# VectorE and ScalarE in program order through the MLP of a transformer block, with the next tokens' normalisation split in three

## The chip, the core and the metric

The kernel runs on one core of a Trainium2 chip. The core has a matmul engine (TensorE, "PE" in the profile; its weight loads stand apart as "PEld"), three engines for elementwise work (VectorE "DVE", ScalarE "ACT", GpSimd "POOL") and SyncE ("SP"), which here only issues transfers. The engines run side by side, each through its own list of instructions in order, and wait for each other on semaphores. The metric is the device time of one execution in microseconds (us), the median of several runs; lower is better. Before the change it is 2831.77 us (three runs, 2831.14 to 2831.92).

## The reference

Two layers on an image of 48 x 48 positions with 768 channels, in float32. The first is a transformer block with 12 heads of attention (with relative positions by row and column) and an MLP with 3072 inner channels; the second goes to frequencies, applies two small complex layers in blocks of 96 channels, and comes back.

```python
xn = layernorm(x); q, k, v = split(xn @ qkv_w + qkv_b)
attn = softmax(q * scale @ k.T + rel_h + rel_w)
x = x + (attn @ v) @ proj_w + proj_b
xn2 = layernorm(x, ln2_g, ln2_b)                 # over the 768 channels
h = gelu(xn2 @ mlp_w1 + mlp_b1)                  # 768 -> 3072
x = x + (h @ mlp_w2 + mlp_b2)                    # 3072 -> 768
xf = rfft2(x); ...; y = irfft2(z) + x            # second layer
```

The change touches the MLP (from `xn2` to the end of the first layer) alone.

## The kernel before

**Tokens and steps.** The 2304 tokens lie in SBUF as 18 tiles of 128 tokens (`x1`, called `main` in the profile). The MLP goes over them in three parts `p` of 768 tokens (`TB`), and in each part over 12 steps `n` of 256 inner channels (`FCH`). Every product of 2 x 2 blocks is computed with seven block products in place of eight (a Winograd form of Strassen's scheme), which needs sums of blocks: of tokens (`sums_of_tokens`, line 179, written to `shared`), of weights (`left` and `right` on GpSimd, lines 161 to 170, `w1s` and `w2s`) and of inner channels (`left` on VectorE, lines 161 to 164, `hs` and a rewritten quarter of `hT`).

**One step on TensorE.** `hidden(p, n)` makes the inner channels of step n: seven products (line 1291) of three matmuls each, into four PSUM banks `h0` to `h3`, cut by `yield` in three pieces of 2, 2 and 3 products. `added(p, n-1, i)` adds the step before to the result for token tiles i = 0, 1, 2: seven products (lines 1355 and 1351) into banks `o0` to `o3`. The two are interleaved: a piece of `hidden(p, n)`, then `added(p, n-1, i)`, three times. Each float32 matmul of this kernel runs as two passes, so the profile has two rows where the code has one call.

**What follows each product.** In `hidden`: a copy `m1` on ScalarE (L1310), the sums `u`, `u7` and `c` on VectorE (L1303, named `u` and `c`), four Gelus on ScalarE (L1297), and then `left` on VectorE (L161 to L164). In `added`, VectorE adds each bank to an accumulator `acc` or to `x1` (L1357, L1359, L1353). Inside one `added`, three banks are used a second time: the fifth product waits until VectorE has read `o0` (the first add), the sixth until it has read `o2` (the third add), the seventh until it has read `o3` (the fourth). The second product needs line 162's result, the third needs line 164's.

**Next tokens.** `normalised(p + 1, i)`, i = 0 to 5, prepares the tokens of the next part: two `bn_stats` (L123) and `bn_aggr` (L125) on VectorE, a square root on ScalarE (L127), a reciprocal (L128) and the scaled copy `hat` (L131) on VectorE, and on GpSimd the second layer's bias is added to `x1` (L1407). In program order the six stand at steps 4 to 9. After step 11, `turned(piece)` transposes a third of the hats on TensorE (L1415) and evacuates them on ScalarE (L1416) ahead of each `added(p, 11, i)`; then come `sums_of_tokens`, the next weights, and `rows_forward(p)` (L1383, `zp`), which starts the second layer's transform.

**Who sets the order.** Through the MLP the order of TensorE, GpSimd and SyncE is that of the program text (`manual_schedule`). VectorE and ScalarE are left to a list scheduler, which places each instruction by priority and by its own costs, and may put it earlier or later than the text has it, across steps and parts. In the built program it does: the six normalisations of part 1 stand at the very start of the MLP, in steps 0 to 2 of part 0, those of part 2 around the end of part 0 (the first statistics of them at the start too), and the pieces of `sums_of_tokens` between the adds of `added(p, 11, 2)`.

```python
work = hidden(p, n)
for i in range(3):
    next(work)
    if n:
        added(p, n - 1, i)
if n < n_f - 1 and (p == 0 or n):
    weights(p, n + 1)
if p < 2 and 4 <= n < 10:
    normalised(p + 1, n - 4)
```

Of the kernel before, what the change touches and what calls it, by code (L numbers as in the profile page):

```python
# [10 lines left out]
F32 = mybir.dt.float32  # L11
F32R = mybir.dt.float32r
I32 = mybir.dt.int32
AF = mybir.ActivationFunctionType
ALU = mybir.AluOpType
# [4 lines left out]
P = 128  # L20
# [3 lines left out]
C = 768  # L24
# [22 lines left out]
def block_then_afno(  # L47
# [27 lines left out]
    nc = tc.nc  # L75
# [10 lines left out]
    eps = const.tile([P, 1], F32, name="eps")  # L86
# [32 lines left out]
    def normalise(pool, src, hat=None, made=None):  # L119

        stats = pool.tile([P, 2, 6], F32, name="stats")
        for i in range(2):
            nc.vector.bn_stats(stats[:, i, :], src[:, ts(i, C // 2)])  # L123
        mv = pool.tile([P, 2], F32, name="mv")
        nc.vector.bn_aggr(mv, stats.rearrange("p a b -> p (a b)"))  # L125
        rstd = pool.tile([P, 1], F32, name="rstd")
        nc.scalar.activation(rstd, mv[:, 1:2], AF.Sqrt, bias=eps)  # L127
        nc.vector.reciprocal(rstd, rstd)  # L128
        if hat is None:
            hat = pool.tile([P, C], F32, name="hat", bufs=4)  # L130
        last = nc.vector.tensor_scalar(hat, src, mv[:, 0:1], rstd, ALU.subtract, ALU.mult)  # L131
        if made is not None:
            made.append(last)
        return hat
# [25 lines left out]
    def left(eng, a11, a12, a21, a22, s):  # L160
        eng.tensor_tensor(s[0], a21, a22, ALU.add)  # L161
        eng.tensor_tensor(s[1], s[0], a11, ALU.subtract)  # L162
        eng.tensor_tensor(s[2], a12, s[1], ALU.subtract)
        eng.tensor_tensor(a21, a11, a21, ALU.subtract)  # L164
# [30 lines left out]
    with ExitStack() as flag_scope:  # L195
# [810 lines left out]
        with tc.If(safe < 1):  # L1006
            with ExitStack() as att:
                xnT = main.rearrange("p (c t) -> p c t", c=NC)
                with tc.tile_pool(name="g_ln1", bufs=3) as ln1, tc.tile_pool(
                    name="g_ps_ln1", bufs=2, space=PSUM  # L1010
                ) as psum:
                    for g in range(T // G):
                        hats = []
# [230 lines left out]
    with ExitStack() as mlp:  # L1244
# [15 lines left out]
        def weights(p, n):  # L1260

            w = wpool.tile([P, NC, FCH], F32, name="w1")
            nc.sync.dma_start(
                out=w, in_=mlp_w1[:, ts(n, FCH)].rearrange("(c p) f -> p c f", p=P)
            )
            ws = wpool.tile([P, 3, 3, P], F32, name="w1s")
            a11, a12, a21, a22 = (w[:, ds(3 * j, 3), ts(i, P)] for i in range(2) for j in range(2))
            left(nc.gpsimd, a11, a12, a21, a22, [ws[:, i] for i in range(3)])
            v = wpool.tile([P, 2, C], F32, name="w2")
            nc.sync.dma_start(  # L1270
                out=v, in_=mlp_w2[ts(n, FCH), :].rearrange("(j p) c -> p j c", p=P)
            )
            vs = wpool.tile([P, 3, CH], F32, name="w2s")
            right(
                nc.gpsimd, v[:, 0, :CH], v[:, 0, CH:], v[:, 1, :CH], v[:, 1, CH:],
                [vs[:, i] for i in range(3)],
            )
            ready_w[p, n] = a11, a12, a21, a22, ws, v, vs

        def hidden(p, n):  # L1280

            a11, a12, a21, a22, ws, v, vs = ready_w.pop((p, n))
            h = hpool.tile([P, 2, TB], F32, name="hT")
            hs = hpool.tile([P, 3, G], F32, name="hs", bufs=1)
            kept[p, n] = h, hs, v, vs

            bank = [psum.tile([P, G], F32, name=f"h{i}") for i in range(4)]

            def product(i, a, b, start):
                for c in range(3):  # L1290
                    nc.tensor.matmul(  # L1291
                        bank[i], a[:, c, :], b[:, c, :],
                        start=(start and c == 0), stop=(c == 2), skip_group_check=not start,
                    )

            def gelu(i, k, src):
                nc.scalar.activation(  # L1297
                    h[:, i, ts(k, G)], src, AF.Gelu, bias=col(V_B1 + 2 * n + i)
                )

            def summed(src, other, name, bufs=2):
                t = upool.tile([P, G], F32, name=name, bufs=bufs)
                nc.vector.tensor_tensor(t, src, other, ALU.add)  # L1303
                return t

            b11, b21, t3, b22, t1, t2, t4 = parts_of_tokens(xt, xs)
            s1, s2, s4 = (ws[:, i] for i in range(3))
            product(0, a11, b11, True)
            m1 = upool.tile([P, G], F32, name="m1")
            nc.scalar.copy(m1, bank[0])  # L1310
            product(1, s2, t2, True)
            u = summed(bank[1], m1, "u")
            yield
            product(2, a21, t3, True)
            u7 = summed(bank[2], u, "u7")
            product(3, s1, t1, True)
            gelu(1, 1, summed(bank[3], u7, "c", 3))
            yield
            product(0, a12, b21, False)
            gelu(0, 0, bank[0])  # L1320
            product(2, a22, t4, False)
            gelu(1, 0, summed(bank[2], u, "c", 3))
            product(3, s4, b22, False)
            gelu(0, 1, summed(bank[3], u, "c", 3))
            left(
                nc.vector, h[:, 0, :G], h[:, 1, :G], h[:, 0, G:], h[:, 1, G:],
                [hs[:, i] for i in range(3)],
            )
            yield
# [3 lines left out]
        def added(p, n, i):  # L1333

            h, hs, v, vs = kept[p, n]
            bank = [psum.tile([P, CH], F32, name=f"o{k}") for k in range(4)]
            if n == 0:
                acc[i] = upool.tile([P, CH], F32, name=f"acc{i}", bufs=1)
            a11, a12, s3, a22 = (
                h[:, f, ds(k * G + i * P, P)] for f, k in ((0, 0), (1, 0), (0, 1), (1, 1))  # L1340
            )
            s1, s2, s4 = (hs[:, k, ts(i, P)] for k in range(3))
            b11, t3, b21, b22 = (v[:, f, ts(k, CH)] for f in range(2) for k in range(2))
            t1, t2, t4 = (vs[:, k] for k in range(3))
            t = 2 * (p * 3) + i
            x11, x12, x21, x22 = (
                x1[:, t + 3 * j, ts(k, CH)] for j in range(2) for k in range(2)
            )

            def product(k, a, b, start, *into):  # L1350
                nc.tensor.matmul(bank[k], a, b, start=start, stop=True, skip_group_check=not start)  # L1351
                for dst in into:
                    nc.vector.tensor_tensor(dst, bank[k], dst, ALU.add)  # L1353

            nc.tensor.matmul(bank[0], a11, b11, start=True, stop=True)  # L1355
            if n == 0:
                nc.vector.tensor_copy(acc[i], bank[0])  # L1357
            else:
                nc.vector.tensor_tensor(acc[i], bank[0], acc[i], ALU.add)  # L1359
            product(1, s2, t2, True, acc[i])  # L1360
            product(2, s3, t3, True, x22)
            product(3, s1, t1, True, x22)
            product(0, a12, b21, False, x11)
            product(2, a22, t4, False, x21)
            product(3, s4, b22, False, x12)
            if n == n_f - 1:
                nc.vector.tensor_tensor(x21, x21, acc[i], ALU.add)
                nc.gpsimd.tensor_tensor(x12, x12, acc[i], ALU.add)
                nc.gpsimd.tensor_tensor(x22, x22, acc[i], ALU.add)
# [29 lines left out]

        hats = {}  # L1400

        def normalised(p, i):

            t = 6 * p + i
            hats[i] = turn.tile([P, C], F32, name="hat2", tag="turn")
            normalise(upool, x1[:, t, :], hats[i])
            nc.gpsimd.tensor_tensor(x1[:, t, :], x1[:, t, :], b2, ALU.add)  # L1407

        def turned(piece):
# [8 lines left out]
                )  # L1418

        weights(0, 0)  # L1420
        for p in range(T // TB):
            for n in range(n_f):
                if (p, n) == (0, 2):
                    nc.sync.dma_start(out=b2, in_=mlp_b2[0, :].partition_broadcast(P))
                    nc.sync.dma_start(out=rows_dft, in_=c_rows)
                work = hidden(p, n)
                for i in range(3):
                    next(work)
                    if n:
                        added(p, n - 1, i)  # L1430
                if n < n_f - 1 and (p == 0 or n):
                    weights(p, n + 1)
                if p < 2 and 4 <= n < 10:
                    normalised(p + 1, n - 4)
            for i in range(3):
                if p < 2:
                    turned(i)
                added(p, n_f - 1, i)
            if p < 2:
                sums_of_tokens(xt, xs)  # L1440
                for n in range(2):
                    weights(p + 1, n)
            rows_forward(p)
        in_order.close()

    with ExitStack() as sp:
# [382 lines left out]
```

## Time and profile before

| what | value |
|---|---|
| median of three runs | 2831.77 us (2831.14 to 2831.92) |
| the profiled execution | 2834.65 us |
| its span, first to last instruction | 2832.9 us |
| TensorE busy in the span | 2788.5 us (98%) |
| VectorE, ScalarE, GpSimd busy | 1700.6, 920.6, 668.7 us |
| mean granted TensorE clock | 0.996 |
| the MLP, first matmul of L1291 to last of L1383 | 1554.4 to 2590.0 us |
| one step of the MLP in the middle of a part | 27.1 us |
| L161 to L164 on VectorE, 144 instructions | 83.3 us busy |
| L1353, adds to `x1` and second adds to `acc` | 358.9 us busy, 556 ns each |

The profile's times are from one execution under the profiler. A row of a timeline gives the start in us from the start of the span, the time from the first start to the last end of the rows merged in it, engine, line, operation, what is written and read, and how many (x). In square brackets stands how long the engine was idle before it and what ended that. The busy end of a matmul is modelled and lies some 0.16 us behind the start of the next one when they follow each other without a gap, so a stall of TensorE is read best from starts: in free running the two passes of a 384 column product take 0.645 us from one product's start to the next.

### The profile page before, as it was taken

To read this page: it belongs to the slowest core of one execution; us is meant where nothing else is said; L and a number is where in the kernel's file an instruction comes from. 1 tells how busy PE (TensorE), PEld (TensorE's weight loads), DVE (VectorE), ACT (ScalarE), POOL (GpSimd) and SP (SyncE) were. 2 spreads that over 40 slices of the span, in tenths; PEclk is the share of its full clock that TensorE was granted. 3 is DMA by queue.
4 is the path that set the end of the run, shared out by engine and by line. 5 is a ranking of instruction groups with operands and counts; after the bars stand their busy time and mean duration, and the time that the engine had idled before them with its cause. 6 is when DMAs were issued, how large, how long until landed. Compare 5 with 4: busy or idle time off the path is not lost. (4 is left out here: it accounts for less than half of the span.)

```text
span 2832.9 us, 41042 instructions
## 1 busy us (share of the span) xinstructions
PE 2788.5 (98%) x15759; PEld 1716.2 (61%) x15759; DVE 1700.6 (60%) x2520; ACT 920.6 (32%) x1466; POOL 668.7 (24%) x662
## 2 busy tenths in 40 slices
PE   8999999999999999999999999999999999999998
PEld 4555655656656565665555555555555555556887
DVE  5434236767676767676756756565565566566665
ACT  1101135656566565665401201131101201102332
POOL 2505010000000000000164233342242422222432
PEclk9999999999999999999999999999999999999999
DMA  4535375273664737455332112131121212123254
GB/s 149 182 103 162 106 158 111 58 133 69 105 126 65 132 64 133 85 82 99 110 132 79 53 65 67 45 101 56 45 67 62 95 45 67 45 70 108 62 162 142
DMA packets 218430, 269.09 MB, mean 95 GB/s; under 512 B 24645, under 2 KB 197053, under 8 KB 216689
## 3 DMA queue, kind: packets, MB, share of 16 engines
q1 hardware_dynamic: 215720, 264.33, 37.5%
q8 instruction: 127, 2.08, 0.3%
q10 hardware_dynamic: 2440, 1.84, 0.2%
q14 instruction: 79, 0.64, 0.1%
q0 software_dynamic: 64, 0.20, 0.0%
HBM read 150.25 MB, written 52.32 MB: 72 GB/s over the span
## 5 line engine op out<-in xcount | busy, mean ns | idle before, releaser
L689 ACT ACTIVATE main<-sp 128x768 f32<-128x768 f32 x648 | 516.3, 812 | 34.5 <-PE sp L679 19.6
L833 DVE TENSOR_TENSOR pairs<-pairs,main 128x1536 f32<-128x1536 f32 x252 | 443.0, 1758 | 27.1 <-DVE pairs L833 0.9
L679 PE MATMUL sp<-terms,select 64*128 64x384 f32 x1296 | 412.0, 629 | 0.0
L1353 DVE TENSOR_TENSOR main<-o,main 128x384 f32<-128x384 f32 x540 | 298.7, 556 | 39.3 <-PE o L1351 1.2
L1291 PE MATMUL h<-shared,w 128*128 128x384 f32 x864 | 296.6, 486 | 0.7 <-POOL w2s L167 0.7
L670 PE MATMUL sp<-shared 64*128 64x384 f32 x1296 | 265.2, 485 | 1.6 <-ACT row_hi L241 1.0
L670 PE MATMUL sp<-qT,kT 64*128 64x384 f32 x1296 | 264.1, 484 | 0.0
L1291 PEld LDWEIGHTS h<-shared,w 128*128 128x128 f32 x864 | 163.9, 190 | 116.1 <-POOL w2s L167 1.3
L735 POOL TENSOR_TENSOR inverse<-inverse,rden 24x32 f32<-24x32 f32 x36 | 15.1, 421 | 926.5 <-DVE sums L734 887.5
L1291 PE MATMUL h<-shared,w1s 128*128 128x384 f32 x648 | 226.6, 486 | 0.0
L1297 ACT ACTIVATE hT<-c,vec 128x384 f32<-128x384 f32 x108 | 66.5, 615 | 465.1 <-DVE c L1303 465.0
L702 PE MATMUL op<-main,shared 128*64 128x384 f32 x1296 | 217.4, 488 | 0.0
L702 PE MATMUL op<-main,v 128*64 128x384 f32 x1296 | 216.4, 488 | 0.0
L833 DVE TENSOR_TENSOR pairs<-main 128x1536 f32<-128x1536 f32 x36 | 63.3, 1758 | 248.1 <-ACT main L689 248.1
L1303 DVE TENSOR_TENSOR c<-h,u 128x384 f32<-128x384 f32 x108 | 60.1, 557 | 212.4 <-PE h L1291 212.4
L1351 PE MATMUL o<-w,hT 128*128 128x384 f32 x432 | 174.8, 487 | 2.4 <-DVE mv L125 2.0
L1351 PE MATMUL o<-w2s,hs 128*128 128x384 f32 x432 | 174.9, 487 | 1.6 <-DVE hs L162 1.6
L679 PEld LDWEIGHTS sp<-terms,select 64*128 64x128 f32 x1296 | 125.3, 186 | 83.7
L1291 PEld LDWEIGHTS h<-shared,w1s 128*128 128x128 f32 x648 | 123.1, 190 | 85.8
L167 POOL TENSOR_TENSOR w2s<-w 128x384 f32<-128x384 f32 x36 | 35.9, 998 | 566.0 <-DMA w<-in_mlp_w_dram 424.0
L529 PE MATMUL m<-main 128*128 128x384 f32 x504 | 164.6, 488 | 2.4 <-DVE main L179 1.8
L702 PEld LDWEIGHTS op<-main,v 128*64 128x64 f32 x1296 | 96.9, 137 | 92.7 <-issue 67.7
(209 smaller groups left out, 4136.6 us busy)
## 6 DMA issues: line engine op xcount, KB each, us to landing
w<-in_mlp_w_dram SPq DMA_DIRECT2D x72, 768.0 KB
terms<-col_parts SPq DMA_DIRECT2D x432, 72.0 KB
terms<-row_hi SPq DMA_DIRECT2D x216, 72.0 KB
terms<-row_lo SPq DMA_DIRECT2D x216, 72.0 KB
main<-in_qkv_w_dram SPq DMA_DIRECT2D x36, 384.0 KB
z<-zt SPq DMA_DIRECT2D x48, 192.0 KB
x<-in_x_blocks_dram SPq DMA_DIRECT2D x18, 384.0 KB
k_d<-o SPq DMA_DIRECT2D x36, 192.0 KB
```

The costliest lines, as they stand in the source:

```text
L167: eng.tensor_tensor(t[0], b12, b11, ALU.subtract)
L529: nc.tensor.matmul(bank, a[:, c, :], b[:, c, :], start=(first and c == 0), stop=(c == 2), skip_group_check=not first,)
L670: nc.tensor.matmul(sp[:, j, :G], kT[at, ts(kt, P)], qT[at, ts(c, G)], start=first, stop=not first,)
L679: nc.tensor.matmul(sp[:, j, :G], select[at, a % 2], ready[pr, c][at, a // 2, b], start=first, stop=not first,)
L689: nc.scalar.activation(p, sp[:, :, :G], AF.Exp, scale=HD**-0.5)
L702: nc.tensor.matmul(op[ts(j, 64)], v[:, kt, ts(j, 64)], exps[:, kt, j, :], start=(kt == 0), stop=(kt == NT - 1),)
L833: nc.vector.tensor_tensor(pairs, so_far, exps[:, ds(kt - 1, 2)], ALU.add)
L1291: nc.tensor.matmul(bank[i], a[:, c, :], b[:, c, :], start=(start and c == 0), stop=(c == 2), skip_group_check=not start,)
L1297: nc.scalar.activation(h[:, i, ts(k, G)], src, AF.Gelu, bias=col(V_B1 + 2 * n + i))
L1303: nc.vector.tensor_tensor(t, src, other, ALU.add)
L1351: nc.tensor.matmul(bank[k], a, b, start=start, stop=True, skip_group_check=not start)
L1353: nc.vector.tensor_tensor(dst, bank[k], dst, ALU.add)
```

## The change

Three edits in the MLP, all of them in the order of work. First, the loop over the parts now stands in `manual_schedule` for VectorE and ScalarE too, so that they run in the order of the text. Second, `hidden` has a fourth piece: `left` on VectorE, which stood ahead of the third `yield`, stands behind it, and `next(work)` is called a fourth time after `added(p, n-1, 2)`; in the text the sums of the inner channels so come behind the adds of the last token tile. Third, `normalised` is cut up: `measured` (statistics, at steps 3 to 8, one tile a step, into one tile `mv6` for all six), one square root for the six at the end of step 8, and from step 9 to 11 two `hat`s a step, the first of them behind one reciprocal for the six. The bias adds on GpSimd go with the hats, two each at steps 9, 10 and 11.

In the built program, TensorE and SyncE have the same instructions in the same order as before. GpSimd has the same instructions, with the twelve bias adds at their new places. VectorE and ScalarE have the order of the text, except that three VectorE instructions of the second layer's setup (L1489 to L1491) still stand among the adds of part 2, where they stood before.

```diff
--- before.py
+++ after.py
@@ -1322,6 +1322,7 @@
             gelu(1, 0, summed(bank[2], u, "c", 3))
             product(3, s4, b22, False)
             gelu(0, 1, summed(bank[3], u, "c", 3))
+            yield
             left(
                 nc.vector, h[:, 0, :G], h[:, 1, :G], h[:, 0, G:], h[:, 1, G:],
                 [hs[:, i] for i in range(3)],
@@ -1399,11 +1400,33 @@
 
         hats = {}
 
+        measures = {}
+
+        def measured(p, i):
+
+            if i == 0:
+                measures[p] = [
+                    upool.tile([P, 6, 2], F32, name="mv6", bufs=1),
+                    upool.tile([P, 6], F32, name="rstd6", bufs=1),
+                ]
+            stats = upool.tile([P, 2, 6], F32, name="stats")
+            for k in range(2):
+                nc.vector.bn_stats(stats[:, k, :], x1[:, 6 * p + i, ts(k, C // 2)])
+            nc.vector.bn_aggr(measures[p][0][:, i], stats.rearrange("p a b -> p (a b)"))
+            if i == 5:
+                mv, rstd = measures[p]
+                nc.scalar.activation(rstd, mv[:, :, 1], AF.Sqrt, bias=eps)
+
         def normalised(p, i):
 
             t = 6 * p + i
+            mv, rstd = measures[p]
+            if i == 0:
+                nc.vector.reciprocal(rstd, rstd)
             hats[i] = turn.tile([P, C], F32, name="hat2", tag="turn")
-            normalise(upool, x1[:, t, :], hats[i])
+            nc.vector.tensor_scalar(
+                hats[i], x1[:, t, :], mv[:, i, 0:1], rstd[:, i : i + 1], ALU.subtract, ALU.mult
+            )
             nc.gpsimd.tensor_tensor(x1[:, t, :], x1[:, t, :], b2, ALU.add)
 
         def turned(piece):
@@ -1418,6 +1441,10 @@
                 )
 
         weights(0, 0)
+        part_by_part = ExitStack()
+        part_by_part.enter_context(
+            tc.manual_schedule(engines={mybir.EngineType.DVE, mybir.EngineType.Activation})
+        )
         for p in range(T // TB):
             for n in range(n_f):
                 if (p, n) == (0, 2):
@@ -1428,10 +1455,14 @@
                     next(work)
                     if n:
                         added(p, n - 1, i)
+                next(work)
                 if n < n_f - 1 and (p == 0 or n):
                     weights(p, n + 1)
-                if p < 2 and 4 <= n < 10:
-                    normalised(p + 1, n - 4)
+                if p < 2 and 3 <= n < 9:
+                    measured(p + 1, n - 3)
+                if p < 2 and n > 8:
+                    for i in range(2 * (n - 9), 2 * (n - 8)):
+                        normalised(p + 1, i)
             for i in range(3):
                 if p < 2:
                     turned(i)
@@ -1441,6 +1472,7 @@
                 for n in range(2):
                     weights(p + 1, n)
             rows_forward(p)
+        part_by_part.close()
         in_order.close()
 
     with ExitStack() as sp:
```

## The prediction

> **What bounds the kernel now.** I read the page first: TensorE is busy 98% of the span, so the change can only win what TensorE loses by waiting, and the question is how much of that lies in the MLP.
>
> ```profile
> PE 2788.5 (98%) x15759; PEld 1716.2 (61%) x15759; DVE 1700.6 (60%) x2520; ACT 920.6 (32%) x1466; POOL 668.7 (24%) x662
> ```
>
> Second, the waits of TensorE between 1554 and 2592 us, the MLP (who waits, for whom, total us, times, longest): little, and nearly all of it for VectorE.
>
> ```profile
> PE o L1351 <- DVE main L1353: 3.5, 5, 1.6
> PE o L1351 <- DVE mv L125: 2.0, 1, 2.0
> PE o L1351 <- DVE hs L162: 1.6, 2, 1.1
> PE h L1291 <- POOL w2s L167: 0.7, 1, 0.7
> PE o L1351 <- DVE hT L164: 0.4, 1, 0.4
> ```
>
> Third, windows from the start of one `added` to the start of what follows it (edges, length, busy us by engine, clock, DMA). An `added` is seven products at 0.645 us, 4.52 us; what a window has over that is lost.
>
> ```profile
> 1571.85:1580.74 8.89, 5.83 (x16) 2.25 (x15) 8.89 (x16) 2.72 (x6) 4.47 (x4) 1.00 0.01 2
> 1877.51:1883.01 5.50, 5.05 (x17) 2.44 (x16) 5.50 (x12) 3.34 (x6) 2.57 (x2) 1.00 0.01 1
> 1884.32:1891.20 6.88, 5.24 (x17) 2.23 (x15) 6.80 (x9) 1.58 (x3) 2.84 (x2) 0.99 0.00 0
> 1891.20:1905.82 14.62, 14.62 (x81) 6.00 (x80) 9.09 (x16) 7.68 (x17) 12.83 (x11) 0.89 0.67 230
> 2230.45:2236.57 6.12, 5.15 (x17) 2.32 (x15) 6.04 (x9) 1.58 (x3) 4.21 (x2) 1.00 0.00 0
> 2236.57:2249.62 13.05, 13.05 (x82) 5.63 (x81) 4.01 (x4) 7.19 (x15) 11.19 (x11) 1.00 0.73 258
> 2546.42:2551.58 5.16, 4.78 (x15) 2.54 (x14) 4.76 (x9) 0.61 (x1) 0.00 (x0) 1.00 0.32 92
> 2561.90:2567.76 5.86, 4.76 (x16) 2.57 (x15) 5.39 (x12) 0.00 (x0) 0.00 (x0) 1.00 0.02 4
> ```
>
> VectorE fills the bad windows: it is late there, not slow on average. Lost, with 0.09 us off where `zp` follows (that step from 0.645 us also costs it with no wait): start 8.89 − 4.52 = 4.4; end of part 0: 1.0 + 2.3; the `zp` run behind it 14.62 − 13.05 = 1.6, at clock 0.89 against 1.00 in part 1; end of part 1: 1.5; part 2: 0.6 + 1.3. Together 12.7 us, the ceiling. Between these, steps follow at 27.1 us without a gap.
>
> **What makes VectorE late.** At the start, hoisted normalisations and `left`, both stretched beside GpSimd's weight sums:
>
> ```profile
> 1571.85 1.23 DVE L162 TENSOR_TENSOR hs<-hs,hT 128x384 f32<-128x384 f32 x1
> 1573.01 1.35 DVE L164 TENSOR_TENSOR hT<-hT 128x384 f32<-128x384 f32 x1
> 1574.28 1.34 DVE L163 TENSOR_TENSOR hs<-hT,hs 128x384 f32<-128x384 f32 x1
> ```
>
> Around the end of part 0, free-running `left` (0.47 us from start to start), hats, and token sums placed in front of adds:
>
> ```profile
> 1870.61 0.56 DVE L161 TENSOR_TENSOR hs<-hT 128x384 f32<-128x384 f32 x1 [0.16 <-PE o L1351]
> 1871.09 0.55 DVE L1353 TENSOR_TENSOR main<-o,main 128x384 f32<-128x384 f32 x1
> 1871.56 0.55 DVE L162 TENSOR_TENSOR hs<-hs,hT 128x384 f32<-128x384 f32 x1
> 1872.02 0.55 DVE L164 TENSOR_TENSOR hT<-hT 128x384 f32<-128x384 f32 x1
> 1872.49 0.55 DVE L163 TENSOR_TENSOR hs<-hT,hs 128x384 f32<-128x384 f32 x1
> ...
> 1877.29 1.94 DVE L131 TENSOR_SCALAR hat<-main,mv,rstd 128x768 f32<-128x768 f32 x2
> 1879.15 0.55 DVE L1359 TENSOR_TENSOR acc<-o,acc 128x384 f32<-128x384 f32 x1
> ...
> 1886.69 1.68 DVE L179 TENSOR_TENSOR shared<-shared 128x1152 f32<-128x1152 f32 x1
> ```
>
> **The change, part by part.** Let T be the end of `added(p, n-1, 2)` on TensorE (1870.34 above).
>
> *Start.* No normalisation is left in steps 0 to 2. Step 0 ends at 1554.36 + 21 x 0.645 = 1567.9; its `c` (0.55), Gelu (0.61) and four `left` (0.47 apart) end near 1571.4, as GpSimd's next weights land (1571.36), and `added(0, 0, 0)`, 6 x 0.645 us behind, needs line 162 at 1572.4. Saves 4.4.
>
> *`left` behind the adds.* In every step the last add (L1353) and L161 change places, as do L163 and L164, so L162 stays at T+1.22 and L164 ends at T+2.70, 0.47 later. TensorE first runs 3.87 us of `hidden` and needs L164 at T+5.16: hidden, with 2.4 us to spare. Without that cover, at the end of part 2, 2561.90 + 2.70 + 0.05 for the semaphore is 0.12 behind the third product's 2564.53; with 0.1, which the trace adds after each stall, +0.2.
>
> *Statistics, steps 3 to 8.* Two L123 and one L125 take 1.1 us (1566.07 to 1567.14), from T+2.6 to T+3.7. Next on VectorE is `u`, due at T+3.98 (1946.72 to 1950.70): nothing. The cover is 0.3 us; a late `u` would push the adds, which have 0.5 to 0.8 us before a bank's second use stalls TensorE.
>
> *One square root, end of step 8.* On ScalarE it waits for the statistics (T+3.7) ahead of `m1`, so `m1` moves from T+2.03 to about T+4.1 and `u` from T+3.98 to T+4.65. The adds start 0.55 late; the first ends at T+5.67 and is needed at T+6.45, the third at T+6.6 and T+7.1. Nothing. Its table load (1.28 us, as in L127's) and Gelu's stand on a ScalarE that has no Gelu before T+12. The ten square roots saved are on an engine 10 to 20% busy: nothing beyond the start.
>
> *Hats, steps 9 and 10.* Reciprocal 0.15 and two hats, 0.67 each when alone, T+2.6 to T+4.0; GpSimd's weight sums come at T+4.8 (1951.55). Nothing. The bias adds (1.80 us each) go on GpSimd behind `w2s`, T+8.8 to T+12.4, ahead of the next `w1s`, then done by T+16.5 and due at T+27.1: nothing.
>
> *Hats, step 11 of parts 0 and 1.* Here TensorE has only 1.31 us of transposes before `added(p, 11, 0)`. Products start at T+1.31, 1.96, then the third waits for L164 (2.75 for 2.63), the fourth at 3.5. Hats run at T+2.62 and T+3.20; the adds follow. What the second hat costs, no row shows exactly: 0.67 alone, 1.36 when GpSimd was already waiting. GpSimd's bias add is released by the first hat's end (T+3.29), when the second has started, which is nearest to the first of two hats at 1895.65, 0.77, which was running when GpSimd's L161 began (1895.96). I take 0.67. The first add ends at T+4.34, so the fifth product starts at 4.39 in place of 4.14; the third add ends at T+5.28, so the sixth at 5.33 in place of 5.13. Sum 0.12 + 0.25 + 0.2 and three times 0.1: 0.9 us an end. With 1.36 it is 1.6. GpSimd's two bias adds then end by T+7.6; the accumulator adds behind them are not needed before `zp`.
>
> By the Trainium skill ("SBUF — State Buffer", section "Who interferes with whom") VectorE and GpSimd hold a shared port pair for a whole instruction, first come first served. By that rule the second hat keeps the pair, 0.67, and the sum is as taken; the stretched rows 1.23 to 1.36 agree with it.
>
> *Token sums.* They now stand behind all adds of `added(p, 11, 2)`: 4 x 1.35 us behind T', its end, due when `hidden(p+1, 0)` needs them, T' + 13.05 + 1.9. Cover 8 us. This frees the adds: the 1.0 + 2.3 and the 1.5 go, for 0.9 each.
>
> *Clock behind the stall.* Between 1891.0 and 1894.4 the granted clock was 0.5, after 1.62 us of idle TensorE; 0.95 us at the end of part 1 and 2.00 at the start brought none. With stalls below 0.4 us I expect none: 1.6 saved. By the skill ("TensorE: Matmul & The Clock Gate", "What's actually happening") the clock falls after an idle window of about 3.4 us; here 1.62 sufficed, so the trace differs, and by the rule alone this saving would not follow and the sum would be 7.0.
>
> *Sum.* 12.7 lost before; after 0 + 0.9 + 0.9 + 2.1 (1.9 and 0.2) is 3.9, so 8.8 saved; I take 8.6 for small change at the seams. The profiled execution had 2834.65, giving 2826.05; it stood 2.88 above the median, which gives 2831.77 − 8.6 = 2823.2. Bounds: no stall at the part ends, −1.8, 2821.4; both second hats at 1.36, +1.4, 2824.6; and if the runs without profiler had no slow clock to lose, +1.6, 2826.2.
>
> **Rivals.**
> (1) *Given back at the part ends* (0.18). Hats at 1.36 and a granted clock of 0.5 behind both: 2 x (0.7 + 1.6) = 4.6, so 2827.8. For: all VectorE work of the end is in one queue. Against: 1.6 us in pieces, in a trace where 0.95 brought no drop.
> (2) *Swallowed* (0.08). Behind the MLP TensorE waits for ScalarE, GpSimd and DMA (chain from 2590 on); if one of these has its own date, the end stays: 2831.8. Against: all of them follow from `zp`, and their order is unchanged.
> (3) *Slower: `left` meets GpSimd* (0.07). Behind the adds, `left` might run beside the weight sums, at 1.25 us: from T+0.75 to T+5.75, 0.6 behind the third product in 33 steps, and with statistics behind it in 12 of them the adds 0.9 more: 33 x 0.6 + 12 x 0.9 = 30.6, so 2854. It decides once GpSimd starts before T+2.7. Against: it starts at T+4.8, when the `w2` transfer that T releases lands; of 144 instructions of `left` only five are stretched, all in a part's step 0, where in parts 1 and 2 a stretched L164 would end at 1923.8 for 1924.8.
> That the order is not the text's is excluded by the built program.
>
> **How the numbers follow.** Forecast 0.67, own range 2821 to 2826. Rivals 0.18, 0.08, 0.07. The range 2820.5 to 2829 leaves out (2), (3) and the tails. What this measurement can tell from no change is about 0.2%, 5.7 us: faster is below 2826.1. Faster 0.72 (the forecast, nearly all, and a part of (1)), same 0.21, slower 0.07.
>
> **What would show it.** Between 1570 and 1582 no idle TensorE; after steps 2 to 10 still none; at the ends of parts 0 and 1 stalls below 0.5 us, waiting for L164 and adds, a second hat near 0.7 us, clock 1.00 in both `zp` runs, L179 behind the last L1368; at the end of part 2 L162's 1.1 us again. Wrong: idle TensorE in the middle steps, L161 to L164 above 1 us, or a longer stretch from the last `zp` to the end.

## The result, and the profile after

| | before | after |
|---|---|---|
| median in the same job, 14 runs each | 2832.05 us (2829.26 to 2834.66) | 2825.16 us (2824.10 to 2827.83) |
| ratio, 95% interval | | 0.9977 (0.9969 to 0.9984) |
| profiled execution, its span | 2834.65, 2832.9 us | 2825.25, 2823.5 us |
| span: up to the first L1291 | 1554.4 us | 1551.8 us |
| span: MLP, first L1291 to the first product of the spectral part (`fp`) | 1036.2 us | 1028.7 us |
| span: from there to the end | 242.3 us | 243.0 us |

The changed kernel is 6.9 us faster by the medians; the interval of the ratio makes that 4.5 to 8.8 us. The forecast was 2823.2 us, 2.0 us lower, with 2825.16 inside its range. The parts of the span show that 7.6 of the profile's 9.4 us lie in the MLP. The other 1.8 are no more than the scatter of code that the change doesn't touch: in three more profiles of the kernel before (below) the stretch ahead of the MLP took 1552.0 to 1553.3 us, and the one behind it 241.5 to 243.1. Of the runs used below, one of e1 (7431.73 us) and one of e8 (10727.41 us) were far slower than the others of their kernel, and the ratios leave them out.

The page of the changed kernel, its busy times. VectorE has 10 instructions less (2520 before) and ScalarE 12 (1466 before); TensorE's share has gone from 98% to 99%:

```profile
PE 2785.1 (99%) x15759; PEld 1715.4 (61%) x15759; DVE 1705.6 (60%) x2510; ACT 914.8 (32%) x1454; POOL 672.0 (24%) x662
```

TensorE's waits in the MLP of the changed kernel (1551 to 2581 us; who waits, for whom, total us, times, longest):

```profile
PE o L1352 <- DVE hs L162: 1.2, 1, 1.2
PE h L1291 <- POOL w2s L167: 0.7, 1, 0.7
...
PE o L1352 <- DVE hT L164: 0.5, 3, 0.2
PE o L1352 <- DVE main L1354: 0.3, 1, 0.3
```

L1352, L1354, L1356 and L1360 are L1351, L1353, L1355 and L1359 of before. The 3.5 us for the adds and the 2.0 us for a normalisation's `mv` are gone; what is left of VectorE's waits stands at the ends of parts. Waits of up to about 0.15 us aren't in the list; they are read from the starts of the products.

Windows of the changed kernel at the same places (edges, length, then busy us of PE, PEld, DVE, ACT and POOL with their instructions, clock, DMA share and GB/s): the first `added` of part 0, the first of the last three at the end of part 0, the two `zp` runs, and the first of the last three at the end of part 2:

```profile
1569.26:1573.77 4.51, 4.51 (x15) 2.66 (x14) 4.14 (x8) 0.00 (x0) 3.32 (x4) 1.00 0.02 4
1864.70:1870.50 5.80, 5.36 (x16) 2.20 (x15) 5.56 (x11) 1.57 (x3) 3.57 (x2) 1.00 0.79 267
...
1882.25:1895.33 13.08, 13.08 (x82) 5.70 (x81) 9.21 (x7) 7.17 (x15) 12.10 (x8) 1.00 0.72 257
2225.81:2238.88 13.07, 13.07 (x82) 5.67 (x81) 9.21 (x7) 7.17 (x15) 12.09 (x8) 1.00 0.75 258
...
2551.28:2557.60 6.32, 4.99 (x15) 2.50 (x14) 5.80 (x12) 0.00 (x0) 0.00 (x0) 1.00 0.01 3
```

At the start TensorE is busy for the whole window, 4.51 us for the 8.89 of before. At the end of part 0 one `added` alone is still long, 5.80 us for a free 4.52: 1.28 lost. Both `zp` runs take 13.1 us at clock 1.00. The end of part 2 is worse than before, 6.32 us for 5.86.

VectorE in the changed kernel around the end of part 0 (start, length, operation):

```profile
1864.06 0.55 DVE L161 TENSOR_TENSOR hs<-hT 128x384 f32<-128x384 f32 x1
1864.64 0.56 DVE L162 TENSOR_TENSOR hs<-hs,hT 128x384 f32<-128x384 f32 x1
1865.24 0.56 DVE L163 TENSOR_TENSOR hs<-hT,hs 128x384 f32<-128x384 f32 x1
1865.71 0.55 DVE L164 TENSOR_TENSOR hT<-hT 128x384 f32<-128x384 f32 x1
1866.18 1.26 DVE L1427 TENSOR_SCALAR hat<-main,mv,rstd 128x768 f32<-128x768 f32 x2
1867.36 0.55 DVE L1360 TENSOR_TENSOR acc<-o,acc 128x384 f32<-128x384 f32 x1
1868.01 0.56 DVE L1354 TENSOR_TENSOR acc<-o,acc 128x384 f32<-128x384 f32 x1
1868.49 2.77 DVE L1354 TENSOR_TENSOR main<-o,main 128x384 f32<-128x384 f32 x5
```

Line 162 reads what 161 wrote, and 163 what 162 wrote: they start 0.58 and 0.60 us apart. Line 164 takes neither's result and starts 0.47 behind. Before, an add stood between 161 and 162, and 164 between 162 and 163, so all four went at 0.47. The second add reads the `acc` that the first wrote and starts 0.65 behind it. In these distances lies the greater part of what the forecast missed at the ends of parts 0 and 1; the account below has the rest.

### The profile page after: what moved, and what is told of

Its sections match the earlier page's. It is cut to its first block, busy times and chain, and to the rows that moved or that the text cites. A ratio compares the mean times of both kernels' runs of the same rounds, so it can differ in the third digit from the quotient of the medians.

```text
span 2823.5 us, 40996 instructions
## 1 busy us (share of the span) xinstructions
PE 2785.1 (99%) x15759; PEld 1715.4 (61%) x15759; DVE 1705.6 (60%) x2510; ACT 914.8 (32%) x1454; POOL 672.0 (24%) x662
## 5 line engine op out<-in xcount | busy, mean ns | idle before, releaser
L833 DVE TENSOR_TENSOR pairs<-pairs,main 128x1536 f32<-128x1536 f32 x252 | 443.1, 1758 | 27.1 <-DVE pairs L833 0.9
L1354 DVE TENSOR_TENSOR main<-o,main 128x384 f32<-128x384 f32 x540 | 299.5, 557 | 43.3 <-PE o L1352 0.5
L1291 PE MATMUL h<-shared,w 128*128 128x384 f32 x864 | 296.6, 486 | 0.7 <-POOL w2s L167 0.7
L1291 PEld LDWEIGHTS h<-shared,w 128*128 128x128 f32 x864 | 164.0, 190 | 116.1 <-POOL w2s L167 1.3
L1291 PE MATMUL h<-shared,w1s 128*128 128x384 f32 x648 | 226.7, 486 | 0.0
L1352 PE MATMUL o<-w2s,hs 128*128 128x384 f32 x432 | 174.9, 487 | 1.2 <-DVE hs L162 1.2
L1352 PE MATMUL o<-w,hT 128*128 128x384 f32 x432 | 175.1, 487 | 0.8 <-DVE hT L164 0.5
L1291 PEld LDWEIGHTS h<-shared,w1s 128*128 128x128 f32 x648 | 123.2, 190 | 85.8
```

What stands on the lines that cost most here:

```text
L833: nc.vector.tensor_tensor(pairs, so_far, exps[:, ds(kt - 1, 2)], ALU.add)
L1291: nc.tensor.matmul(bank[i], a[:, c, :], b[:, c, :], start=(start and c == 0), stop=(c == 2), skip_group_check=not start,)
```

## The experiments

Each kernel was timed beside the kernel before on the same chip. Differences of 1 or 2 us drown in the spread of the runs, so they are read from the MLP's length (first L1291 to first `fp`) and from the waits.

| kernel | median us | ratio to before, 95% | MLP us |
|---|---|---|---|
| before (four profiles) | 2831.5 to 2832.5 | 1 | 1036.2, 1036.6, 1035.0, 1036.4 |
| after | 2825.16 | 0.9977 (0.9969 to 0.9984) | 1028.7 |
| e1, order without the split | 2829.79 | 0.9988 (0.9979 to 0.9998) | 1033.6 |
| e2, split without the order | 2833.01 | 1.0004 (0.9995 to 1.0013) | 1034.0 |
| e4, L164 ahead of L163 | 2824.79 | 0.9976 (0.9966 to 0.9986) | 1028.0 |
| e5, hats a step earlier | 2823.07 | 0.9972 (0.9960 to 0.9983) | 1027.1 |
| e6, e4 and e5 | 2822.23 | 0.9965 (0.9952 to 0.9978) | 1026.0 |
| e7, sums at their old place | 2911.79 | 1.0279 (1.0266 to 1.0292) | 1110.6 |
| e8, sums behind the fourth add | 2823.97 | 0.9968 (0.9956 to 0.9980) | 1027.0 |
| e9, token sums ahead of the adds | 2839.10 | 1.0025 (1.0016 to 1.0035) | 1042.1 |
| e10, sums behind the fifth add | 2822.00 | 0.9968 (0.9955 to 0.9980) | 1025.8 |

**e1: the order without the split.** Each normalisation whole, as before, at steps 4 to 9.

```diff
-                if p < 2 and 3 <= n < 9:
-                    measured(p + 1, n - 3)
-                if p < 2 and n > 8:
-                    for i in range(2 * (n - 9), 2 * (n - 8)):
-                        normalised(p + 1, i)
+                if p < 2 and 4 <= n < 10:
+                    normalised(p + 1, n - 4)
```

> Program order and the sums one place later, but each of the twelve normalisations whole again, at steps 4 to 9, with its own square root and table load. T is the end of a step's last group of products on TensorE. If the order alone brings the gain, the stretch of the MLP (first L1291 to the first product of the spectral part) is that of the changed kernel, 1028.7 us, less up to 1.8 us, since no hats are left in step 11: 2823 to 2826 us. Theory: VectorE now stands in its queue until the square root behind the last statistics has come (statistics to T+3.9, table load 1.28, square root 0.2, so the hat runs from about T+5.3 to T+6.0 and u, due at T+4.0, ends near T+6.6); the first add is then 0.3 to 1.2 us behind the point where TensorE needs its bank, in each of the 12 steps: 4 to 14 us more than the changed kernel, 2829 to 2839 us, and idle TensorE within steps 4 to 9 of parts 0 and 1 that waits for VectorE's adds or u.

Measured: MLP 1033.6 us, 4.9 more than the changed kernel. The start has no wait, the ends of parts 0 and 1 lose 0.49 us, and of the twelve steps ten lose 0.41 us, the other two 0.76 and 1.19 (in the one of 1.19 the hat takes 1.38 us beside GpSimd's weight sums, for 0.68 in the rows below). VectorE of e1 in such a step (brackets: idle before it, and what ended that):

```profile
1706.07 1.01 DVE L123 BATCH_NORM_STATS2 stats<-main 128x6 f32<-128x384 f32 x2
1707.12 0.21 DVE L125 BATCH_NORM_AGGREGATE mv<-stats 128x2 f32<-128x12 f32 x1
1707.69 0.16 DVE L128 RECIPROCAL rstd<-rstd 128x1 f32<-128x1 f32 x1 [0.36 <-ACT rstd L127]
1707.89 0.68 DVE L131 TENSOR_SCALAR hat<-main,mv,rstd 128x768 f32<-128x768 f32 x1
1708.48 0.55 DVE L1303 TENSOR_TENSOR u<-h,m 128x384 f32<-128x384 f32 x1
```

The theory's mechanism holds: the queue stands still for the square root, then `u` and all adds follow the hat. Its size is at the low end, because the table load isn't in the way: ScalarE does it at 1700.19, right behind the last Gelu, and then waits 5.89 us for the statistics.

**e2: the split without the order.** The three lines that put VectorE and ScalarE in program order are left out.

```diff
-        part_by_part = ExitStack()
-        part_by_part.enter_context(
-            tc.manual_schedule(engines={mybir.EngineType.DVE, mybir.EngineType.Activation})
-        )
```

> The normalisation in three steps and the sums one place later, but VectorE and ScalarE left to the planner, without program order. The built order has the statistics of parts 1 and 2 and six hats in the first two steps of part 0, hats of part 2 around the end of part 0, pieces of the token sums (L179) among the adds, and L164 ahead of L163. If the split and the later sums bring the gain, the time is that of the changed kernel, 2825 us. Theory: program order is what removes the losses, so they come back: some 4 us or more at the start of part 0 (VectorE full with statistics and hats before line 162), and 1 to 3.3 us at each end of parts 0 and 1: MLP 1034 to 1040 us, time 2830 to 2836 us.

Measured: 2833.01 us, no different from before; MLP 1034.0 us. TensorE's waits in e2 (1556 to 2576 us):

```profile
PE o L1352 <- DVE main L1354: 4.0, 5, 1.6
PE o L1352 <- DVE hs L162: 1.8, 2, 1.5
PE o L1352 <- DVE acc L1358: 0.8, 1, 0.8
```

The waits of before are back, as expected. So neither half carries the gain: order alone takes some 2.5 us off the MLP (1036.0 is the mean of before's four), the split alone 2.0, both together 7.4. Of e2's 2.0 a part is the clock: half clock fell in the MLP in three of the four profiles of before and not in e2, and against b2, where it didn't fall either (1035.0), e2 is 1.0 us shorter. The order needs the split so that the queue doesn't wait for a square root in twelve steps, and the split needs the order to stay where it is written.

**e4: line 164 ahead of line 163.**

```diff
-            left(
...
+            nc.vector.tensor_tensor(hs[:, 0], a21, a22, ALU.add)
+            nc.vector.tensor_tensor(hs[:, 1], hs[:, 0], a11, ALU.subtract)
+            nc.vector.tensor_tensor(a21, a11, a21, ALU.subtract)
+            nc.vector.tensor_tensor(hs[:, 2], a12, hs[:, 1], ALU.subtract)
```

> The changed kernel with line 164 ahead of line 163 inside the sums of inner channels, so that an operation that doesn't depend on its predecessor stands between two that do. In the changed kernel's trace the four start 0.58 to 0.60 us apart where one takes the other's result, and 0.47 where not. Theory: the four take 3 x 0.47 + 0.6, line 164 ends near T+2.3 in place of T+2.87, and the third product at the ends of parts 0 and 1 no longer waits for it (0.34 us and some 0.1 behind it): the losses of 1.28 us there fall to about 0.9, because what stands behind (hats, adds) comes 0.1 to 0.2 earlier too, and the end of part 2 loses 0.2 to 0.4 us less. In all 1 to 1.5 us, 2824 us. Rival: the spacing is not due to the dependence, or the adds set the end anyway: the sums keep their length, nothing changes, 2825 us. The time alone hardly tells them apart; the starts of L161 to L164 and the windows at the ends of the parts do.

VectorE of e4 at the end of part 0 (L1327 to L1330 are the four sums, L1329 the old 164):

```profile
1865.09 0.55 DVE L1327 TENSOR_TENSOR hs<-hT 128x384 f32<-128x384 f32 x1
1865.67 0.56 DVE L1328 TENSOR_TENSOR hs<-hs,hT 128x384 f32<-128x384 f32 x1
1866.15 0.55 DVE L1329 TENSOR_TENSOR hT<-hT 128x384 f32<-128x384 f32 x1
1866.61 0.55 DVE L1330 TENSOR_TENSOR hs<-hT,hs 128x384 f32<-128x384 f32 x1
1867.08 1.26 DVE L1428 TENSOR_SCALAR hat<-main,mv,rstd 128x768 f32<-128x768 f32 x2
```

The spacing is due to the dependence: 0.58, then 0.48 and 0.46. The rival is out there. But the loss only moved. The waits of e4:

```profile
PE o L1353 <- DVE hs L1328: 1.2, 1, 1.2
PE o L1353 <- DVE acc L1361: 0.8, 2, 0.4
PE o L1353 <- DVE main L1355: 0.5, 2, 0.4
```

No product waits for the old line 164 any more; the fifth waits for the first add, behind the hats, 0.57 us instead of 0.28. An end loses 1.16 for 1.28, and of the expected 1 to 1.5 us the MLP shows 0.7 (0.34 and 0.08 of it at the end of part 2).

**e5: hats a step earlier.** Statistics at steps 2 to 7, hats at 8 to 10, none at step 11.

```diff
-                if p < 2 and 3 <= n < 9:
-                    measured(p + 1, n - 3)
-                if p < 2 and n > 8:
+                if p < 2 and 2 <= n < 8:
+                    measured(p + 1, n - 2)
+                if p < 2 and 8 <= n < 11:
```

> The changed kernel with statistics at steps 2 to 7 and hats at steps 8 to 10, so that no hat is left in step 11. Theory: the fifth and sixth product at the ends of parts 0 and 1 waited because two hats (1.3 us with the reciprocal's start) stand ahead of the adds; without them the first add runs at about T+3.0 and TensorE loses only the third product's wait for L164, 0.34 us and 0.1: each end 1.28 -> 0.45, 1.7 us in all, 2823.5 us. Nothing is lost in steps 2 to 10. Rival: the adds are late for another reason (their own 0.47 us chain behind line 163), and the ends keep 1 us or more each: 2825 us.

Measured: MLP 1027.1, 1.6 us less (expected 1.7); each end loses 0.49, at line 164 alone. The third to sixth product of e5's `added(0, 11, 0)`: the third waits, and behind it none does.

```profile
1867.15 0.88 PE L1352 MATMUL o<-w,hT 128*128 128x384 f32 x2 [0.18 <-DVE hT L164]
1867.87 0.81 PE L1352 MATMUL o<-w2s,hs 128*128 128x384 f32 x2
1868.52 0.81 PE L1352 MATMUL o<-w,hT 128*128 128x384 f32 x2
1869.16 0.81 PE L1352 MATMUL o<-w2s,hT 128*128 128x384 f32 x2
```

**e6: both.** The edits of e4 and e5.

> Line 164 ahead of line 163 and the hats at steps 8 to 10, together. In e4 the swap alone took away the third product's wait (0.34 us) but the fifth then waited 0.57 in place of 0.28, behind the hats: 1.14 lost for 1.26. In e5 the hats alone left 0.49, all of it at the third product. Theory: each wait was hidden by the other, so the two together bring more than the sum of e4's 0.12 and e5's 0.77 an end: about 0.1 us is left at each end of parts 0 and 1, and the end of part 2 loses the third product's 0.34: the MLP takes 1026.0 us (e5: 1027.1, e4: 1028.0), time 2822 us. Rival: the two gains simply add or overlap, ends at 0.3 us or more, 1026.8 us. What remains is 1.3 to 1.8 us at the end of part 2, where line 162 follows the last add.

Measured: MLP 1026.0 us, as the theory had it, and 0.08 us lost at each end of parts 0 and 1. By the windows an end lost 1.28 with neither edit, 1.16 with e4's, 0.49 with e5's, 0.08 with both: two waits in a row on one engine, each covered by the other. Time 2822.23 us.

**e7: the sums at their old place.** Program order, but `left` ahead of the last group's adds; two buffers for the sums.

```diff
-            hs = hpool.tile([P, 3, G], F32, name="hs", bufs=1)
+            hs = hpool.tile([P, 3, G], F32, name="hs", bufs=2)
...
-            yield
             left(
...
-                next(work)
```

> The changed kernel with the sums of inner channels at their old place in the text, ahead of the adds of the last group of products (with two buffers for the sums, which that place needs). E is the end of the fourth quarter of the hidden products. Theory: program order alone would be bad there: line 161 waits for the last Gelu (E + 1.46), and the adds stand behind the four sums, so the first add ends at E + 4.15 where the fifth product wants its bank at E + 2.58: about 1.6 us there, 0.31 at the sixth and 0.1 behind each, 2.1 us in each of 33 steps, 69 us: 2894 us; up to 2947 us if the granted clock falls behind each stall, which cost 1.6 us once in the trace of the kernel before. Rival: the place of the sums is of no matter, as TensorE has work of the next step: 2825 us.

Measured: 2911.79 us. VectorE of e7 in one step:

```profile
1621.09 0.56 DVE L161 TENSOR_TENSOR hs<-hT 128x384 f32<-128x384 f32 x1 [0.68 <-ACT hT L1297]
...
1622.76 0.55 DVE L164 TENSOR_TENSOR hT<-hT 128x384 f32<-128x384 f32 x1
1623.22 0.55 DVE L1359 TENSOR_TENSOR acc<-o,acc 128x384 f32<-128x384 f32 x1
```

VectorE waits 0.68 us for the Gelu with ready adds behind it, and the fifth product starts at 1623.83, 1.6 us late. Each of the 33 steps takes 29.29 us in place of 27.1. Three steps of e7 in a row, from one fifth product to the next:

```profile
1740.97:1770.25 29.28, 27.64 (x84) 15.71 (x84) 17.40 (x33) 2.90 (x5) 7.84 (x8) 1.00 0.17 54
1770.25:1801.22 30.97, 29.32 (x84) 16.46 (x84) 17.49 (x33) 4.18 (x6) 7.86 (x8) 0.94 0.17 52
1801.22:1830.51 29.29, 27.64 (x84) 15.71 (x84) 17.40 (x33) 4.41 (x7) 7.86 (x8) 1.00 0.16 54
```

The middle one has the same stall and the same work, but a clock of 0.94 and 1.68 us more. The clock's records show half speed for 3.41 us behind 8 of the 33 stalls. 33 x 2.19 + 8 x 1.68 = 85.7 us; the ends of the parts, where the sums are early, lose some 4.6 less than in the changed kernel; that makes 81, and 82.0 were measured. The place of the sums is a part of the change that the order can't do without.

**e8 and e10: the sums between the last adds.** Hats as in e5, two buffers for the sums, and `left` inside `added(p, n-1, 2)`, in e8 behind its fourth add and in e10 behind the fifth:

```diff
-        def added(p, n, i):
+        def added(p, n, i, between=None):
...
             product(3, s1, t1, True, x22)
+            if between is not None:
+                next(between)
             product(0, a12, b21, False, x11)
...
-                        added(p, n - 1, i)
-                next(work)
+                        added(p, n - 1, i, work if i == 2 else None)
+                if n == 0:
+                    next(work)
```

```diff
             product(0, a12, b21, False, x11)
+            if between is not None:
+                next(between)
             product(2, a22, t4, False, x21)
```

> Hats at steps 8 to 10, and the sums of inner channels between the fourth and the fifth add of the last group of products (two buffers for the sums): behind the last Gelu, ahead of the last three adds, which nothing but the next group of products waits for. Theory: at the end of part 2, line 162 is then done before the last group follows, so its 1.15 us and the third product's 0.34 go; at the ends of parts 0 and 1 the third product waits no more; in the middle steps the last three adds come 2.1 us later and are covered by 3.87 us of hidden products, and u, due at T + 4, is not late. MLP 1027.1 (e5) - 1.8 - 0.8 = 1024.5 us, time 2820.5 us. Rival: the three late adds push u and with it the adds of the next group, 0.2 to 0.5 us in 33 steps: 7 to 16 us more, 2830 to 2839 us.

> As e8, but the sums of inner channels stand behind the fifth add of the last group in place of the fourth. In e8 the wait at the end of part 2 only moved: the next group's first product waited 1.72 us for its bank, whose last add stood behind the sums, where e6 loses 1.16 us at line 162. Theory: behind the fifth add that bank is free in time, line 162 ends before the last group's products stop, and only the sixth add's bank is some 0.1 to 0.2 us late: the end of part 2 loses 0.1 to 0.3 us, the ends of parts 0 and 1 nothing, the middle steps nothing: MLP 1024.7 us (e6: 1026.0), time 2821 us. Rival: another bank or line 164 is late by as much, 1026 us or more, 2822 to 2823 us.

Measured: MLP 1027.0 and 1025.8 us, for 1024.5 and 1024.7 expected. Both lose nothing in the middle steps, so e8's rival is out, but at the end of part 2 the wait moved to the bank whose add now stands behind the sums. TensorE of e8 there, first product of the last group:

```profile
2551.75 0.88 PE L1356 MATMUL o<-w,hT 128*128 128x384 f32 x2 [1.72 <-issue]
```

and of e10, third product:

```profile
2551.42 0.88 PE L1352 MATMUL o<-w,hT 128*128 128x384 f32 x2 [0.65 <-DVE main L1354]
```

In e8 the bank's add is the first of the three that follow the sums (2551.10, from VectorE's rows), which the trace doesn't name as the releaser. In e10 I had allowed 0.1 to 0.2 us and it was 0.81. The times, 2823.97 and 2822.00, aren't told apart from e6's.

**e9: token sums ahead of the adds.**

```diff
                     turned(i)
+                    if i == 2:
+                        sums_of_tokens(xt, xs)
                 added(p, n_f - 1, i)
             if p < 2:
-                sums_of_tokens(xt, xs)
```

> The changed kernel with the sums of tokens (four of 1.35 us alone, 8.39 us in all beside GpSimd in the changed kernel's trace) ahead of the adds of the last group of step 11 in parts 0 and 1, where the planner had put a part of them. Theory: the adds start only when these are done, 6.5 to 9.5 us into the group; the fifth product, wanted at 2.6 us, waits 4 to 7 us at both ends, 8 to 15 us in all: 2833 to 2840 us, and the granted clock falls to 0.5 for 3.4 us behind each stall, which costs up to 1.6 us more each. Rival: the sums wait for the last transposes anyway and the adds are needed late: below 2 us an end, 2826 to 2829 us, and the losses before the change came from the hats alone.

VectorE of e9 at the end of part 0:

```profile
1877.68 6.80 DVE L179 TENSOR_TENSOR shared<-shared 128x1152 f32<-128x1152 f32 x4
1884.39 0.55 DVE L1360 TENSOR_TENSOR acc<-o,acc 128x384 f32<-128x384 f32 x1
1885.05 0.56 DVE L1354 TENSOR_TENSOR acc<-o,acc 128x384 f32<-128x384 f32 x1
1885.52 1.72 DVE L1354 TENSOR_TENSOR main<-o,main 128x384 f32<-128x384 f32 x3
```

The fifth product starts at 1885.00, after 4.50 us of idle TensorE, and as much at part 1. MLP 13.4 us longer, time 2839.10 us: as the theory had it. The records have half clock for 3.41 us from 1884.60 and for 6.83 us from 2232.76, from within the first and the second stall (1880.50 to 1885.00 and 2230.30 to 2234.80) to some us behind it. Where the token sums stand in VectorE's queue is worth several us an end.

**b1, b2, b3: the kernel before, profiled again.** Unchanged.

> The kernel before, profiled again. In its first profile TensorE idled 1.62 us at the end of part 0 within one stretch of 3.41 us of the clock's records, and ran the next one at half clock; with the records of e7, where 33 equal stalls of 1.64 us gave 8 stretches of half clock, theory: the clock falls only where a stall lies whole within one stretch, so in about half of the profiles of before, and where it doesn't the run of zp behind the stall takes 13.05 us, not 14.6. Rival: it falls each time, 14.6 us, and all of the 1.6 us belongs to the saving.

> As b1: half clock behind the stall at the end of part 0 in about one profile of two by theory (zp 13.05 or 14.6 us), in each by the rival.

> As b1 and b2: half clock behind the stall at the end of part 0 in about one profile of two by theory (zp 13.05 or 14.6 us), in each by the rival.

Windows from the first `zp` of part 0 to about the end of the last one. b1:

```profile
1889.65:1903.90 14.25, 14.25 (x81) 5.93 (x80) 8.75 (x16) 7.66 (x17) 12.79 (x11) 0.91 0.68 236
```

b2:

```profile
1890.07:1903.40 13.33, 13.22 (x81) 5.82 (x80) 9.17 (x16) 7.31 (x17) 11.47 (x10) 1.00 0.72 252
```

b3, with the start of part 0 ahead of it:

```profile
1572.00:1580.50 8.50, 6.28 (x13) 2.92 (x14) 7.54 (x17) 1.58 (x2) 2.13 (x2) 0.80 0.01 2
1890.19:1903.60 13.41, 13.29 (x81) 5.83 (x81) 9.17 (x16) 7.35 (x17) 11.54 (x10) 1.00 0.72 251
```

TensorE idled 1.62 to 1.63 us ahead of `zp` in all three. In b1 the clock fell behind it, as in the first profile; in b2 and b3 it didn't; in b3 it fell at the start of part 0 instead, behind the stall there. That is two of four for this place, and three of four with any. The rival, that it falls each time, is out. e2 says the same: an idle time of 1.62 us at the same place, and clock 1.00. The theory's 13.05 us for a `zp` run without the fall isn't what b2 and b3 show: it takes 13.4, as TensorE waits once more in it, for a copy on ScalarE (0.11 to 0.12 us idle).

## Why the prediction was right, and where it was off

What remained was put at 3.9 us of the 12.7; it is 5.1 (twice 1.28, and 2.57 at the end of part 2), and the saving in the profile's MLP 7.6 in place of 8.6. The mechanism was the one forecast; the sizes at the ends of the parts were too small.

| step of the prediction | forecast | measured |
|---|---|---|
| start | nothing lost | nothing lost |
| sums behind the adds, middle steps | nothing | nothing |
| statistics, one square root, hats at steps 9 and 10 | nothing | nothing |
| end of L164 after T (1863.39) | T + 2.70 | T + 2.87 |
| two hats at step 11 | 2 x 0.67 | 1.26 from first start to last end |
| ends of parts 0 and 1 | 0.9 each | 1.28 each |
| third add's end behind the first's, step 11 | 0.94 | 1.13 |
| end of part 2, all waits | 2.1 | 2.57 |
| token sums hidden | 4 x 1.35 us, 8 us of cover | 8.39 us beside GpSimd, done at 1891.69, 3.6 us ahead of `hidden` at 1895.30 |
| clock behind the ends | no fall | no fall |

**The mis-sized term is the distance of dependent instructions on VectorE, that of `left` first.** I read 0.47 us from start to start off before's rows, where another instruction stood between each dependent pair, and kept it for an order in which they stand back to back. Line 164 so ends 0.17 us later than forecast, and the hats and adds behind it start as much later. The adds hold a dependent pair of their own: the first two write `acc`, and they start 0.65 apart (1867.36 and 1868.01), where I had 0.47. It is not the bank that the second waits for: in e9 all banks had been ready for 4 us, and the two start 0.65 apart too (1884.39 and 1885.05), the next one 0.47 behind.

A second size was wrong. Between the end of what a product waits for and its start I allowed 0.05 us. The sixth product has that (1869.04 to 1869.09), but the third and the fifth start 0.15 behind (1866.26 to 1866.41, 1867.91 to 1868.06). Before's rows have both values, 0.15 at the end of part 2 alone; which of them a product gets, the runs don't show.

Together the third, fifth and sixth product start 0.27, 0.28 and 0.37 us behind the forecast. As waits these are 0.34 us for 0.12, 0.28 for 0.25 and 0.31 for 0.2; behind each the trace adds 0.08 to 0.10, as forecast. With 0.08 behind the second product that is the 1.28 of an end. At the end of part 2 line 162 costs 1.39 for 1.34, line 164 0.41 for 0.2, and a further 0.16 stands in the `added` before. e4 shows the dependence as the cause of the spacing. It also shows that `left` alone isn't the whole error: with its sums 0.47 apart again from the second on, an end still loses 1.16, not 0.9, since the hats, the pair of adds and the 0.15 stand as they were.

**The chosen values that held.** The second hat was taken as 0.67, not 1.36: GpSimd's bias add started at 1866.93, when the second hat already ran (from 1866.77, 0.67 us). That agrees with the Trainium skill ("SBUF — State Buffer", "Who interferes with whom": the port pair belongs to whoever came first, for a whole instruction). At the start, and once in each later part, L164 took 1.35 us beside GpSimd, with TensorE not waiting. The cover of 0.3 us ahead of `u` was rightly called thin: in e1 an idle 0.36 and a hat in it cost 0.41 a step.

**The clock.** That no half clock would be left was right. But its 1.6 us were counted whole against the median of the runs, while the fall is in two of four profiles at that place, and in three of four at any in the MLP. Nor are they the fall alone: without it that `zp` run took 13.4 us in b2 and b3, so the fall cost 0.9 (b1) to 1.2 us. A part of the 1.7 us by which the medians' saving (6.9) fell short of the forecast (8.6) may be here; how often the runs without profiler had the fall, no record shows.

**The rivals.** (1), given back at the ends, had the right place and not the right causes: 1.28 lies between the forecast's 0.9 and its 1.6 for both hats at full length, but none of its clock loss came. (2), swallowed behind the MLP: the stretch behind it is 243.0 us for 241.5 to 243.1 before. (3), `left` beside GpSimd, didn't occur in the middle steps. Program order can make this kernel slower, but for another reason: with the sums ahead of the adds (e7) it costs 79 us against before.

## What to carry to other kernels

When an engine is put in program order, read its queue for every instruction that waits for another engine, and ask what ready work stands behind it: the square root (e1), the Gelu (e7) and the token sums (e9) made the MLP 4.9, 82.0 and 13.4 us longer than the changed kernel's by standing in the wrong place. A duration from start to start belongs to the neighbours it was read between; when an edit brings dependent instructions next to each other, it has to be read again. Where two waits lie one behind the other on one engine, repairing one shows little (e4: 0.12 us an end), and only both show what they were worth (e6: 1.20).

Of the versions run, e6 and e10 are the fastest by their medians, 2822.2 and 2822.0 us; they aren't told apart from each other. Both still wait at the end of part 2: in e6 TensorE idles 1.16 us for line 162, in e10 0.65 us for a bank's add.

## What the runs showed of the hardware

- The granted clock falls in stretches of 3.41 us (or multiples) whose phase isn't tied to the kernel: the stall of 1.62 us ahead of `zp` lies whole within one stretch in the first profile of before and in b1, and a boundary cuts it in b2 (1.36 us of it behind the boundary) and in b3 (0.71 us behind it). With TensorE's idle time summed over each such stretch (from its rows and the clock's records, inside the MLP), half clock followed no stretch with up to 1.58 us of idle, each with 2.04 or more, and some of those between: in e7 eight stretches of 1.64 to 1.65 us were followed by it, others of 1.62 to 1.65 weren't, nor was one of 1.78 in b2. A stall of about 1.6 us that a boundary cuts in two cost nothing more; one that lay within a stretch cost up to 1.68 us. The Trainium skill ("TensorE: Matmul & The Clock Gate", "What's actually happening") has the free-running window of 3413 ns, and the runs agree; it has the fall after an idle window, and here stretches that were idle for about half of their time were sometimes enough.
- Two dependent VectorE sums of 128 x 384 from SBUF start 0.58 to 0.60 us apart, independent ones 0.46 to 0.48. Two adds from PSUM into the same `acc` start 0.65 apart (after, e9).
- A product that waits for VectorE starts 0.05 us behind the end of what it waits for in some places and 0.15 in others (after: 1869.09 and 1866.41); the runs don't show what decides it.
- The table load of e1's square root took place ahead of the wait, not behind it (load at 1700.19, square root at 1707.36).
